# Layer 0 attention with the scores made twice: turned score products, maxima subtracted inside the product, sums from the value product

## The chip, the cores and the metric

The program runs on one core of a Trainium2 chip. Its time is the device time of one execution in microseconds (us). A core has TensorE (PE, whose weight loads are listed as PEld), VectorE (DVE), ScalarE (ACT), GpSimd (POOL) and SyncE (SP, which only starts transfers here). Each works through its own queue in order, and they meet at semaphores.

## What is computed

The reference is a stack of four layers, each `x + attention(norm(x)) + ffn(norm(x))`, on x of 4 batches of 256 rows of 512 values. Only layer 0's attention, and one small step of layer 1, are touched:

```python
q, k, v = (proj(wq), proj(wk), proj(wv))        # 32 heads of 16 values
q = _apply_rope(q, sin, cos)                    # x * cos + rot * sin
k = _apply_rope(k, sin, cos)
scores = jnp.einsum('bnth,bnsh->bnts', q, k) * (1.0 / math.sqrt(h))
scores = jnp.where(causal, scores, -jnp.inf)
attn = jax.nn.softmax(scores, axis=-1)
out = jnp.einsum('bnts,bnsh->bnth', attn, v)
out = out.transpose(0, 2, 1, 3).reshape(B, T, C)
return jnp.einsum('btc,dc->btd', out, wo)
```

Layer 1 needs for its "bind" vectors the mean magnitude of two small weight vectors per head (`alpha = mean(abs(w))`).

## The kernel before

Everything is in float32. A float32 product is two matrix instructions and two weight loads in the trace, so that a count of x8 there is four products.

**Blocks.** `layer0_attention` (L151) takes one batch of 256 rows after the other. In a batch, queries and keys stand as features on the partitions: four blocks of 128 features, that is 8 heads each, a pair of heads (e = 0 and 1) in each group of 32 partitions. There are 16 blocks. `kT` holds the keys twice, once with the features of the other head of each pair set to zero (`eo`, L286 and L287), so that one product with 32 contraction rows gives the scores of both heads of a pair; four such products, in the four row groups of the array, run together (L357). The causal mask makes three quarters of a square of scores: "part 1" is the lower 128 query rows against 256 keys, "part 0" the upper 128 against 128 keys.

**A head's path.** DVE adds the mask, negates and takes the minimum in one pass from PSUM to SBUF (`masked`, L379, which gives the negated maximum `nm`). ACT takes the exponential in place, with the sum of each row (L393). DVE inverts the sums (L404), POOL multiplies by them (L406), PE turns three 128x128 squares so that keys stand on the partitions (L417), DVE or ACT copies them out of PSUM (`keys`, L98 and L96), and PE multiplies by the values (L430), one group of 32 columns of the array for each pair, `v` having zeros in the columns of the other head. ACT copies the result of e = 0 to `oT` (L442) and DVE adds that of e = 1 (L444). Per block there are 8 such heads.

**Features.** For each block of queries and of keys: four products (L260), two multiplications with the rotary tables on DVE (L271), a product with a signed permutation `swap` that exchanges the two halves of a head (L275), an addition on DVE (L282), and for keys the two masked copies (ACT L286, DVE L287). Values are products L303, the output projection L327, the addition to x L337.

**Order.** The queues of PE, DVE, ACT and POOL are written by hand: a loop over slots h, 8 to a block, issues what is due, some of it through `at(h, ...)`. Features, values and the norm of the next batch (`turn`) are spread over the slots of the current one. `aside` holds 64 small pieces, one for each odd slot: the unpacking of the gate and up weights of layer 0's feed-forward part (L563 to L599, DVE, with transfers from SP). PSUM has 8 banks: 4 for scores (tag A), 2 for the turned squares (T), 2 for halves that everything else takes in turn (`hb`, L200).

**Layer 1's step.** At the end of layer 0's feed-forward part, `binding` (L811) fills a 128x128 square with ones on POOL (L815), takes magnitudes on ACT (L817) and adds them over the partitions with a product on PE (L819). On POOL's queue the fill stands behind two multiplications of the norm (L835).

Of the kernel before, what the change touches and what calls it, by code (L numbers as in the profile page):

```python
# [30 lines left out]
P = 128  # L31
# [24 lines left out]
def block_stack(ctx: ExitStack, tc: tile.TileContext, d: dict, out: bass.AP):  # L56
# [94 lines left out]
    def layer0_attention(hook, aside):  # L151
# [6 lines left out]

        with (
# [3 lines left out]
            psum_banks("ps_a0", A=4, T=2, H=2),  # L163
# [7 lines left out]
            swap = load(wp, "swap0", eng=nc.scalar)  # L171
# [9 lines left out]
            for i in range(2):  # L181
                v = wp.tile([P, 2, 2, L0_PAIRS, 32], F32, name=f"v0_{i}")
                nc.gpsimd.memset(v, 0.0)
                vbuf.append(v)
            hook()
# [8 lines left out]
            for t in range(2):  # L194
                turned(t, xns[t])
# [47 lines left out]
            class Batch:  # L243


                def __init__(self, b):
# [3 lines left out]
                    self.oT = ap.tile([P, NC, T], F32, tag="oT", name=f"oT_{b}")  # L250
                    self.v = vbuf[b % 2]

                def features(self, h, qk, blk):
# [18 lines left out]

                    def rotate():
                        had["rot"] = hb()
                        nc.tensor.matmul(had["rot"], lhsT=swap, rhs=had["qs"], start=True, stop=True)  # L275

                    def add():
                        if qk == 0:
                            dst = self.qT[:, blk, :]
                        else:  # L280
                            dst = had["kk"] = ap.tile([P, T], F32, tag="kk", name="kk" + name)
                        nc.vector.tensor_tensor(dst, had["rot"], had["qc"], ALU.add)  # L282

                    def split():
                        dst, kk = self.kT[:, blk], had["kk"]
                        nc.scalar.activation(dst[:, 0, :], kk, AF.Copy, scale=eo[:, 0:1])  # L286
                        nc.vector.tensor_scalar(dst[:, 1, :], kk, eo[:, 1:2], None, ALU.mult)  # L287
# [3 lines left out]
                    at(h + 3, rotate)  # L291
                    at(h + 4, add)
                    if qk:
                        at(h + 5, split)
# [49 lines left out]
            class Block:  # L344


                def __init__(self, u, blk):
                    self.u, self.blk = u, blk
                    self.p, self.keys = [], []

                def scores(self, part):
# [3 lines left out]
                    self.s = [ps("A", [P, 2, n], f"s{part}_{self.blk}_{i}") for i in range(4)]  # L355
                    for r, s in zip(rows, self.s):
# [8 lines left out]
                def masked(self, part, i):  # L365

                    if part:
                        self.p.append(
                            [
                                smp.tile([P, 2, T], F32, tag="p1", name="p1"),  # L370
                                smp.tile([P, 2, P], F32, tag="p0", name="p0", bufs=7),
                                smp.tile([P, 2, 2], F32, tag="nm", name="nm"),
                                smp.tile([P, 2, 2], F32, tag="sums", name="sums"),
                                smp.tile([P, 2, 2], F32, tag="rs", name="rs"),
                            ]
                        )
                    p1, p0, nm, _, _ = self.p[i]
                    for e in range(2):
                        nc.vector.tensor_tensor_reduce(  # L379
                            out=(p1 if part else p0)[:, e, :],  # L380
                            in0=self.s[i][:, e, :],
# [5 lines left out]
                            accum_out=nm[:, e, part : part + 1],  # L387
                        )

                def exponentials(self, e, i):  # L390
                    p1, p0, nm, sums, _ = self.p[i]
                    for part, p in ((1, p1), (0, p0)):
                        nc.scalar.activation(  # L393
                            p[:, e, :],
                            p[:, e, :],
                            AF.Exp,
                            bias=nm[:, e, part : part + 1],
                            scale=-1.0,
                            accum_out=sums[:, e, part : part + 1],
                        )  # L400

                def normalise(self, e, i):
                    p1, p0, _, sums, rs = self.p[i]
                    nc.vector.reciprocal(rs[:, e, :], sums[:, e, :])  # L404
                    for part, p in ((1, p1), (0, p0)):
                        nc.gpsimd.tensor_tensor(  # L406
                            p[:, e, :],
                            p[:, e, :],
                            rs[:, e, part : part + 1].to_broadcast([P, p.shape[2]]),
                            ALU.mult,  # L410
                        )

                def transpose(self, e, i):
                    p1, p0 = self.p[i][:2]
                    tp = ps("T", [P, 3, P], "pT")
                    for k, src in enumerate((p0[:, e, :], p1[:, e, 0:P], p1[:, e, P:T])):
                        nc.tensor.transpose(tp[:, k, :], src, ident)  # L417
                    self.turned = tp

                def copied(self, e, i):  # L420
                    self.keys.append(smp.tile([P, 3, P], F32, tag="keys", name="keys"))
                    evac(i, self.keys[-1], self.turned)

                def values(self, e):

                    v = self.u.v
                    av = hb()
                    for k, cols, of in ((0, slice(0, T), slice(0, 2)), (1, slice(P, T), slice(2, 3))):
                        for i, r in enumerate(rows):
                            nc.tensor.matmul(  # L430
                                av[r, cols],
# [1762 lines left out]
```

## Time and profile before

| | |
|---|---|
| Median of 3 runs | 1456.17 us (1454.14 to 1458.66) |
| The profiled execution | 1458.98 us, span of its instructions 1457.1 us, mean granted TensorE clock 0.983 |
| Layer 0 attention | from the start to 301.0 us, where the first instruction of the feed-forward part (ACT L685) starts |
| Busy in the first 300 us | PE 262.2, DVE 209.8, ACT 164.2, POOL 133.9 us |
| Busy in the whole span | PE 1381.7, DVE 910.3, ACT 571.1, POOL 737.1 us |
| Layer 1's step | PE waits 3.97 us before L819, at 455.94 us |

A row of a group of instructions has the line, the engine, the operation, output and inputs by the program's names with their shapes, the count, busy time and mean duration of one, and the idle time of the engine just before them with what ended it. Neighbouring instructions of an engine overlap at their ends: in a dense stretch the distance from start to start is less than the mean duration, and the timeline shows it. A row of the timeline has start, duration, engine, line, operation, shapes and a count of merged instructions; a bracket gives the wait before it.

### The profile page before, as it was taken

What the parts mean: (1) busy time and instruction counts of PE and PEld (TensorE: products, weight loads), DVE (VectorE), ACT (ScalarE), POOL (GpSimd) and SP (SyncE); (2) the same over time, 40 slices, a digit from 0 to 9 for tenths busy, and PEclk for the clock granted to TensorE, in tenths of its full rate; (3) what the DMA queues carried; (4) which work ended last, traced back from release to release, by engine and by line L of the source; (5) the groups of instructions that cost most, each with busy time, mean ns of one, the idle gap of its engine ahead of it and who ended that gap; (6) DMA issues with size and microseconds to landing.
All of it is one profiled execution on the core that took longest, in us unless ns stands there. A gap on an engine that the chain in (4) does not pass through costs nothing.

```text
span 1457.1 us, 21158 instructions
## 1 busy us (share of the span) xinstructions
PE 1381.7 (95%) x7204; PEld 1085.1 (74%) x7204; DVE 910.3 (62%) x2482; ACT 571.1 (39%) x1717; POOL 737.1 (51%) x790
## 2 busy tenths in 40 slices
PE   7988989899998999999999999999999999989998
PEld 4656656578644657887887888888888788777887
DVE  5687777768844437745556765566565555857654
ACT  2565656768401222312332333323333233445430
POOL 1354535657751204755575776857757666310200
PEclk9999999999999999999999999999999999999999
DMA  5021112220250002210121202211022010302001
GB/s 191 1 57 34 42 30 42 59 75 1 69 144 0 15 0 89 64 45 24 61 88 42 75 26 65 89 48 62 23 87 87 29 30 0 131 1 109 1 1 58
DMA packets 50958, 76.23 MB, mean 52 GB/s; under 512 B 16491, under 2 KB 23942, under 8 KB 50466
## 3 DMA queue, kind: packets, MB, share of 16 engines
q1 hardware_dynamic: 49778, 73.77, 16.8%
q8 instruction: 57, 0.93, 0.3%
q10 hardware_dynamic: 960, 0.85, 0.2%
q0 software_dynamic: 112, 0.26, 0.1%
q14 instruction: 51, 0.42, 0.1%
HBM read 66.96 MB, written 7.91 MB: 51 GB/s over the span
## 4 chain that ended last, share of the span: by engine, by line
PE 79%; DVE 13%; ACT 3%; issue 2%; POOL 1%; DMA 1%; SPq 0%; ACTq 0%; DVEq 0%; POOLq 0%
PE m L1301 15%; PE m L1265 14%; PE dn L665 5%; PE gu L699 4%; PE half L260 4%; PE s L1645 4%; PE av L1718 4%; PE m L1287 3%; PE m L1277 3%; PE s L357 2%; PE pT L417 2%; PE s L1649 2%; PE l1o L948 2%; PE av L1719 2%; PE half L327 2%
## 5 line engine op out<-in xcount | busy, mean ns | idle before, releaser
L1693 POOL TENSOR_TENSOR p<-p,rs 128x512 f32<-128x512 f32 (+1 forms) x128 | 107.5, 860 | 242.8 <-DVE rs L1690 242.8
L406 POOL TENSOR_TENSOR p<-p,rs 128x256 f32<-128x256 f32 (+1 forms) x256 | 129.2, 529 | 156.6 <-DVE rs L404 131.3
L1711 ACT COPY q<-pT 128x512 f32<-128x512 f32 x64 | 37.5, 585 | 280.5 <-PE pT L1702 280.5
L1679 ACT ACTIVATE p<-p,nm 128x256 f32<-128x256 f32 (+1 forms) x256 | 113.3, 451 | 54.4 <-DVE nm L1663 54.4
L1690 DVE RECIPROCAL rs<-sums 128x4 f32<-128x4 f32 x64 | 11.4, 178 | 178.2 <-ACT p L1679 177.9
L393 ACT ACTIVATE p<-p,nm 128x256 f32<-128x256 f32 (+1 forms) x256 | 113.6, 449 | 0.9 <-DVE nm L379 0.9
L1265 PE MATMUL m<-xT,wq_b 128*128 128x256 f32 x448 | 103.9, 380 | 4.4 <-DVE x_sb L1515 3.0
L379 DVE CUSTOM_DVE_ANT_0 p<-s,cmask 128x256 f32<-128x256 f32 (+1 forms) x256 | 79.0, 347 | 38.2 <-PE s L357 33.8
L1265 PEld LDWEIGHTS m<-xT,wq_b 128*128 128x128 f32 x448 | 82.1, 190 | 14.8 <-DVE x_sb L1515 3.4
L1248 POOL TENSOR_TENSOR c<-c,z 128x512 f32<-128x512 f32 x28 | 36.4, 1298 | 111.0 <-DVE c L1247 41.7
L1301 PE MATMUL m<-wo_b,o 128*128 128x256 f32 x384 | 90.2, 381 | 0.0
L1317 POOL TENSOR_TENSOR q<-q,t 128x512 f32<-128x512 f32 x64 | 85.2, 1333 | 6.1 <-DVE t L1316 6.1
L1316 DVE TENSOR_TENSOR t<-m,rope_sb 64x512 f32<-64x512 f32 (+1 forms) x144 | 86.3, 600 | 1.9
L1350 DVE TENSOR_TENSOR x_sb<-x_sb,m 128x512 f32<-128x512 f32 x82 | 54.5, 680 | 50.8 <-PE m L1301 40.7
L665 PE MATMUL dn<-wd,hT 128*128 128x512 f32 x176 | 80.6, 619 | 2.3 <-DVE sb L714 2.3
L1663 DVE CUSTOM_DVE_ANT_0 p<-s,cmask 128x256 f32<-128x256 f32 (+1 forms) x256 | 76.1, 353 | 10.6 <-PE s L1645 8.3
L1265 PE MATMUL m<-x_s,wq_t 128*128 128x256 f32 x320 | 78.4, 391 | 3.3 <-DVE x_sb L1350 2.2
L417 PE MATMUL pT<-ident,p 128*128 128x128 f32 x384 | 66.0, 288 | 15.6 <-ACT keys L96 6.6
L1301 PEld LDWEIGHTS m<-wo_b,o 128*128 128x128 f32 x384 | 70.8, 190 | 10.8 <-DVE t L1316 2.3
L1727 ACT COPY o<-av 128x512 f32<-128x512 f32 x64 | 37.6, 588 | 90.9 <-PE av L1719 90.7
L417 PEld LDWEIGHTS pT<-ident,p 128*128 128x128 f32 x384 | 44.9, 145 | 36.8 <-POOL p L406 21.1
L1265 PEld LDWEIGHTS m<-x_s,wq_t 128*128 128x128 f32 x320 | 61.7, 196 | 13.4 <-DVE x_sb L1350 2.6
(322 smaller groups left out, 3557.9 us busy)
## 6 DMA issues: line engine op xcount, KB each, us to landing
wq_b<-in_wq SPq DMA_DIRECT2D x38, 256.0 KB
wo_b<-in_wo SPq DMA_DIRECT2D x32, 256.0 KB
raw<-in_wo SPq DMA_DIRECT2D x16, 512.0 KB
wkv_b<-in_wkv SPq DMA_DIRECT2D x16, 256.0 KB
wos_d<-wos_row SPq DMA_DIRECT2D x28, 128.0 KB
gate_q<-in_gate_q SPq DMA_DIRECT2D x11, 256.0 KB
up_q<-in_up_q SPq DMA_DIRECT2D x11, 256.0 KB
wq3s_b<-in_wq SPq DMA_DIRECT2D x8, 256.0 KB
```

The costliest lines, as they stand in the source:

```text
L379: nc.vector.tensor_tensor_reduce(out=(p1 if part else p0)[:, e, :], in0=self.s[i][:, e, :], in1=cmask if part else cmask[:, P : 2 * P], sc ...
L393: nc.scalar.activation(p[:, e, :], p[:, e, :], AF.Exp, bias=nm[:, e, part : part + 1], scale=-1.0, accum_out=sums[:, e, part : part + 1],)
L406: nc.gpsimd.tensor_tensor(p[:, e, :], p[:, e, :], rs[:, e, part : part + 1].to_broadcast([P, p.shape[2]]), ALU.mult,)
L417: nc.tensor.transpose(tp[:, k, :], src, ident)
L665: nc.tensor.matmul(po, lhsT=hT[:, k, t * P : (t + 1) * P], rhs=wd[:, k, :], start=k == 0, stop=k == NBLK - 1,)
L1265: nc.tensor.matmul(out[:, i, :], lhsT=b[:, c, i * P : (i + 1) * P], rhs=a[:, c, :], start=start and i == 0 and c == 0, stop=i == 1 and c == 1,
L1301: nc.tensor.matmul(out[:, t, :], lhsT=a[:, c, t * P : (t + 1) * P], rhs=b[:, c, :], start=start and t == 0 and c == 0, stop=t == 1 and c = ...
L1316: nc.vector.tensor_tensor(t2[at], src[of], sin[of], ALU.mult)
L1317: after(1, lambda: nc.gpsimd.tensor_tensor(dst, dst, t2, ALU.add))
L1663: nc.vector.tensor_tensor_reduce(out=x[f"p{part}"][:, e, :], in0=x[f"s{part}"][:, e, :], in1=cmask if part else cmask[:, P : 2 * P], scale ...
L1679: nc.scalar.activation(p, p, AF.Exp, bias=x["nm"][:, part, e : e + 1], scale=-1.0, accum_out=x["sums"][:, part, e : e + 1],)
L1693: nc.gpsimd.tensor_tensor(p, p, bc(x["rs"][:, part, :], 2, n), ALU.mult)
```

## The change

The exponentials are no longer taken in the layout in which the maxima are found. Scores are still made as before, but only for their maxima; then they are made a second time with keys on the partitions, less the maxima, and the exponential of that is what the value product takes.

- The two `masked` passes (DVE) remain, but their output is thrown away (tile `masked`); the negated maximum goes to a column of one of three 128x256 tiles `maxima`, at row 16 of a pair's 32 for head 0 and at row 0 for head 1.
- `widened`: ACT makes `q_e`, the block's queries twice, each with the other head's features set to zero (2 x 128x256); POOL makes `k_e`, the keys `kT` with a one added in row 16 (head 0) or row 0 (head 1) of each 32 (128x512).
- `turn_maxima`: PE turns the two 128x128 squares of maxima into one half; `lowered`: DVE puts them, by a mask, into the free row of `q_e` (2 x 128x256). The product of `k_e` and `q_e` then is score less maximum.
- `turned`: for each e four products of 256 columns and four of 128 in the four row groups, into four PSUM tiles of 128x384. `exponentials`: one ACT pass 128x384 from PSUM for each head, straight into `keys`. `selected`: POOL sets the entries above the diagonal to zero (two 128x128 squares in one instruction per head).
- The value buffers are filled with ones instead of zeros, so the value product gives the row sums in the columns of the other head. `gathered` takes by a mask the outputs (`o_e`) and the sums, on ACT for e = 0 (2 x 128x256) and on DVE for e = 1 (2 x 128x256). `inverted`: DVE inverts 128x256 sums and exchanges the 16s of each 32 with a stream shuffle; `normalised`: POOL multiplies (128x256). The per-head reciprocal, multiplication, three squares and copy are gone.
- The rotary exchange is a stream shuffle on DVE (128x256) instead of the product with `swap`, whose load is gone; the signs move to the table; the addition moves from DVE to POOL; the second masked copy of keys moves from DVE to ACT.
- PSUM: six banks for scores of both kinds (A=6), none for squares. Each block takes 16 banks from A instead of 8.
- The loop is written anew: offsets of a block's steps from its slot 8n are in two tables, features of the next batch keep their slots, three of batch 0's features and its values move a few slots, and the outputs of batches 1 and 2 are put together after slot 106 (of 134), those of batch 3 at the end. The 64 pieces of `aside` still go to the odd slots from 1.
- In layer 1 the fill with ones and the magnitudes move from `binding` to `values_binding`, where they are issued earlier on POOL and ACT.

```diff
-            psum_banks("ps_a0", A=4, T=2, H=2),
+            psum_banks("ps_a0", A=6, H=2),
...
-                nc.gpsimd.memset(v, 0.0)
+                nc.gpsimd.memset(v, 1.0)
...
+                        nc.vector.stream_shuffle(had["rot"], had["qs"], [i ^ 8 for i in range(32)])
...
-                        nc.vector.tensor_tensor(dst, had["rot"], had["qc"], ALU.add)
+                        nc.gpsimd.tensor_tensor(dst, had["rot"], had["qc"], ALU.add)
...
+                        for e in range(2):
+                            nc.scalar.activation(dst[:, e, :], kk, AF.Copy, scale=eo[:, e : e + 1])
...
+                def widened(self):
+                    for e in range(2):
                         nc.scalar.activation(
+                            self.q[:, e, :], self.u.qT[:, self.blk, :], AF.Copy, scale=eo[:, e : e + 1]
                         )
+                    nc.gpsimd.tensor_tensor(
+                        self.k, self.u.kT[:, self.blk], bc(eo[:, 2:4], 2, T), ALU.add
+                    )
...
+                def lowered(self):
+                    for e in range(2):
+                        q = self.q[:, e, :]
+                        nc.vector.scalar_tensor_tensor(
+                            q, self.maxT, eo[:, 2 + e : 3 + e], q, ALU.mult, ALU.add
+                        )
...
+                def turned(self, e):
+                    self.st = [ps("A", [P, 3, P], f"st_{self.blk}_{i}") for i in range(4)]
+                    for k, of in ((0, slice(0, 2)), (1, slice(2, 3))):
+                        for r, s in zip(rows, self.st):
+                            nc.tensor.matmul(
+                                s[:, of, :],
+                                lhsT=self.k[r, e, k * P : k * P + P],
+                                rhs=self.q[r, e, k * P : T],
+                                start=True,
+                                stop=True,
+                            )
+                def exponentials(self, i):
+                    self.keys.append(smp.tile([P, 3, P], F32, tag="keys", name="keys", bufs=9))
+                    nc.scalar.activation(self.keys[-1], self.st[i], AF.Exp)
+                def selected(self, e, i):
+                    k = self.keys[4 * e + i][:, 0:3:2, :]
+                    nc.gpsimd.affine_select(
...
+                def inverted(self):
+                    nc.vector.reciprocal(self.sums, self.sums)
+                    nc.vector.stream_shuffle(self.sums, self.sums, [i ^ 16 for i in range(32)])
...
+            first = {
+                -10: lambda x: x.scores(1),
+                -6: lambda x: x.scores(0),
+                -3: lambda x: x.turn_maxima(),
+                -2: lambda x: x.lowered(),
+                0: lambda x: x.turned(0),
+                4: lambda x: x.turned(1),
+                6: lambda x: x.values(0),
+                7: lambda x: x.gathered(0),
+                10: lambda x: x.values(1),
+                11: lambda x: x.gathered(1),
+                13: lambda x: (x.inverted(), x.normalised()),
+            }
+            then = {
+                -9: lambda x: (x.masked(1, 0), x.masked(1, 1)),
+                -8: lambda x: x.masked(1, 2),
+                -7: lambda x: (x.masked(1, 3), x.widened()),
+                -5: lambda x: (x.masked(0, 0), x.masked(0, 1)),
+                -4: lambda x: (x.masked(0, 2), x.masked(0, 3)),
+            }
...
+            self.full = lp.tile([P, P], F32, name="full")
+            nc.gpsimd.memset(self.full, 1.0)
+            self.mag = lp.tile([P, 2, H], F32, name="mag")
+            nc.scalar.activation(self.mag, w["bqk"], AF.Abs)
             self.vbind = signs(lp, w["bv"], alpha, [P, H, P], "v").rearrange("p h d -> p (h d)")
...
-            full = lp.tile([P, P], F32, name="full")
-            nc.gpsimd.memset(full, 1.0)
-            mag = lp.tile([P, 2, H], F32, name="mag")
-            nc.scalar.activation(mag, w["bqk"], AF.Abs)
```

## The prediction, as put on record before the changed kernel ran

> **What bounds the kernel now.** I read the page first (PE 95% busy), then busy times by stretches of 20 us, then the groups by shape, the waits and the timeline. Layer 0 attention ends at 301.0 us, where ACT L685 starts. Its stretches, with columns start:end, length, busy PE, PEld, DVE, ACT, POOL, granted clock, DMA share, GB/s:
>
> ```profile
> 140.00:160.00 20.00, 18.70 (x137) 13.42 (x130) 16.25 (x77) 13.02 (x51) 10.27 (x20) 1.00 0.19 42
> 160.00:180.00 20.00, 18.53 (x145) 12.91 (x145) 15.49 (x75) 12.09 (x51) 10.31 (x21) 1.00 0.18 38
> 180.00:200.00 20.00, 17.09 (x115) 12.20 (x114) 12.13 (x56) 10.39 (x40) 7.66 (x16) 0.91 0.17 40
> ```
>
> PE leads, DVE follows at three quarters, DMA is idle. What PE does is in the groups of the first 460 us:
>
> ```profile
> L406 POOL TENSOR_TENSOR p<-p,rs 128x256 f32<-128x256 f32 x128 | 79.2, 619 | 156.6 <-DVE rs L404 131.3 <-PE pT L417 15.4 <-ACT v L314 4.7
> ...
> L417 PE MATMUL pT<-ident,p 128*128 128x128 f32 x384 | 66.0, 288 | 15.6 <-ACT keys L96 6.6 <-DVE keys L98 6.4 <-DVE rs L404 0.8
> ...
> L404 DVE RECIPROCAL rs<-sums 128x2 f32<-128x2 f32 x128 | 19.8, 154 | 2.3 <-ACT p L393 2.1
> ...
> L275 PE MATMUL half<-qs,swap_sb 128*128 128x256 f32 x64 | 19.6, 388 | 1.4 <-DVE qT L282 0.9 <-DVE qc L271 0.4
> ```
>
> PE spends 66 us on squares and waits for their POOL, DVE and ACT neighbours; POOL waited 157 us. Because instructions overlap, I cost them from start to start, from PE's timeline:
>
> ```profile
> 153.97 1.14 PE L357 MATMUL s<-kT,qT 32*128 32x512 f32 x8
> 155.05 0.86 PE L430 MATMUL half<-keys,v 128*32 128x256 f32 x16
> 155.84 1.21 PE L417 MATMUL pT<-ident,p 128*128 128x128 f32 x6
> 156.88 1.89 PE L260 MATMUL half<-xT,wq_sb 128*128 128x256 f32 x8
> 158.61 0.49 PE L417 MATMUL pT<-ident,p 128*128 128x128 f32 x3
> ```
>
> So: scores of part 1 take 1.07 (155.05 less 153.97), of part 0 (the row at 161.63, next at 162.27) 0.64, a value product 0.79, a square 0.165 to 0.173 (six in 1.04), a full product of four 1.73. In the same way DVE: a masked pass 0.345 (256) or 0.21 (128), an operation 128x256 with a PSUM input 0.33, a keys copy 0.47, a small reciprocal 0.08. POOL: 0.97 for L406's two; ACT: 0.38 for a copy of 384 from PSUM, 0.40 to 0.42 for a pass over 256.
>
> **PE per block.** Removed: 24 squares 3.96 and two swap products 0.87. Added: the second scores. Their 256-column groups are part 0's, 0.64. Four of 128 columns are not in the trace; 1.07 less 0.64 is 0.43 per 256 columns, so 0.64 less 0.21 gives 0.43 (ends 0.35, half of a value product's rest, and 0.64). Twice 1.07 makes 2.14, two squares of maxima 0.33. Net -2.4, from 15.3 to 13.0 on average.
>
> **DVE per block.** Removed: 8 reciprocals 0.64, 4 copies 1.88, 2 rotary additions 0.66, one masked key copy 0.27, oT 0.33: 3.8. Added: `lowered` 0.66, `gathered` 0.66, three shuffles, one reciprocal over 256. A shuffle is not in the trace; the nearest row, L287 with SBUF on both sides, has 0.27: I take 0.30 (ends 0.27 and 0.47, a copy of 384). The reciprocal is the large unknown. At the low end it is like any pass over 256, 0.33. But its own rows grow: 128x2 154, 128x4 178, 128x8 203 ns, that is 6 to 8 ns an element where a tensor operation from 128x4 (153) to 128x8 (167) has about 3. Over 256 that makes 1.6 to 2.2; I take 1.9. Added 4.1, net +0.3, from 12.1 to 12.4. DVE comes level with PE.
>
> **ACT and POOL.** ACT loses 8 x 0.88 and 4 x 0.38 and the oT copy, and gains 8 exponentials from PSUM at about 0.43, q_e 0.84, a key copy 0.42, gathered 0.74: from some 10 to 7. POOL loses 8 x 0.97 and gains 8 selections, the nearest row being
>
> ```profile
> L931 POOL TENSOR_SCALAR_AFFINE_SELECT a<-a 128x256 f32<-128x256 f32 x16 | 6.9, 453 | 31.9 <-ACT a L930 31.9
> ```
>
> so 3.6, k_e 1.3 (L1033, 128x512) and three operations of 0.6: 6.7. Here a rule of the Trainium skill speaks against the change: "GPSIMD Engine Reference", section "4.1 Engine selection", wants elementwise work on VectorE and not on GpSimd, which is slower for two inputs. The rows agree on the price (619 against 416 ns of L282). By the rule the three operations would stay on DVE, 1.0 more in each of 16 blocks; by the rows POOL has half its time free, and a feature is wanted two slots later or more. I go with the rows: cost nothing. Were POOL late, `split` would wait on ACT, with exponentials queued behind it and PE's next scores waiting for their bank.
>
> **The sum by intervals.** Work is uneven: features and values (1.73 on PE; 0.96 or 0.2 on DVE) fall on odd slots of some blocks, on top of 5.8 on PE and 8.0 plus 2.1 of weight pieces on DVE for each. I cut both queues of the changed program where a block's first part-1 scores stand, for intervals 1 to 14 (PE/DVE): 10.8/9.7, 11.6/12.0, 7.5/10.0, 10.9/11.8, 13.3/13.4, 13.3/13.2, 12.7/11.6, 12.7/11.9, 13.3/13.0, 13.3/13.9, 7.5/10.4, 10.9/11.8, 12.7/11.0, 9.2/11.3. The larger sum to 170. The same method on the kernel before gives 209, while the trace has 237 (about 28.5 to 266.0): 28 more, of which some 12 is clock (the share not granted, times length, over the stage) and 16 is handing over, 1.2 an interval.
>
> Handing over after: walking one feature block by hand, in order, PE first waits 0.9 for the masked passes before the squares of maxima, but DVE then sets the pace: 14.0 against 13.9. A block with one product takes about 11 against 10.1, as exponentials on ACT and bank releases bind. There are fewer hops than before but two equal queues; I take 1.0, 14 in all.
>
> Clock: here the Trainium skill and the trace part. Rows (as above):
>
> ```profile
> 114.00:116.00 2.00, 0.40 (x2) 0.15 (x2) 2.00 (x9) 0.01 (x1) 0.97 (x2) 1.00 0.04 8
> 116.00:118.00 2.00, 1.83 (x9) 1.55 (x10) 0.70 (x6) 1.35 (x6) 0.97 (x2) 0.71 0.45 137
> 118.00:120.00 2.00, 2.00 (x6) 1.32 (x4) 0.00 (x0) 0.77 (x4) 0.00 (x0) 0.50 0.37 60
> ```
>
> PE was thin, not idle, and the clock fell to half. "TensorE: Matmul & The Clock Gate", "Part 1: The HAM clock gate", has it fall after an idle window of some 3.4 us. By that rule the new stage, whose waits are near 1 us, loses nothing; by the rows each thin stretch costs about 2.5. Thin are intervals 3, 11 and 14: 7.5.
>
> Start: without swap products in between, the four first features end near 19.5; keys are ready by 19.6 (end of the second feature 16.1, rotary 1.0, a norm statistic 0.7, POOL 0.6, two ACT copies 0.8, handovers 0.4), so first scores at 20.3 for 23.2, interval 0 takes 10.7: 31. Tail from the last block's scores: before 35 us for 29.7 of PE work. After 29.3, but the end is a chain: last values, gathered 0.7, reciprocal and shuffle 2.2, POOL 0.6, then output products 6.9 and addition: 35 again. The weight pieces keep their slots, and their transfers with them; DVE waited 0.8 for the first (`gate_q`, started at 77.3, taken at 82.7), and with slots a fifth shorter may wait 1 to 2 there, which PE's slack in interval 3 mostly covers. Stage end: 31 + 170 + 14 + 7.5 + 35 = 257.5, a gain of 43.5.
>
> **Layer 1's fill.**
>
> ```profile
> 435.50 16.47 PE L665 MATMUL dn<-wd,hT 128*128 128x512 f32 x38
> 455.94 0.59 PE L819 MATMUL alpha<-mag,full 128*128 128x8 f32 x2 [3.97 <-POOL full L815]
> 456.39 7.97 PE L665 MATMUL dn<-wd,hT 128*128 128x512 f32 x12
> ...
> 465.07 5.32 PE L665 MATMUL dn<-wd,hT 128*128 128x512 f32 x12
> ```
>
> The fill stood behind two POOL multiplications; issued earlier it lies among the weight additions before 421 us, and ACT is idle for 52 us before 444. PE saves 3.97, and the next twelve run in 5.32 for 7.97: 6.6. Late next would be the squares of the normed rows, ready at 453.0, wanted at 457.5: nothing. Low end 4.0. After layer 0 all orders else are the same and PE is the bound, so gains pass on.
>
> Profiled execution: 1458.98 less 50.1 is 1408.9. It lies 2.8 above the median; so 1406.
>
> **Rivals.** (a) The reciprocal costs 0.33: PE alone binds, intervals sum to 162, the tail loses 1.6, together 9 less: 1397. For it: no row above 8 elements; against it: the slope. (b) Handing over costs twice as much, 2.2 an interval and 4 in the tail: the ring of six banks makes each group of four scores wait for two banks that DVE frees and two that ACT frees, four times a block, and PE and DVE have no slack for each other. 21 more: 1427. For it: before, PE with slack on DVE lost 1.2; against it: the walk. (c) Slower: half-filled, row-tiled scores now make up more of PE's work, and the clock stays low. To lose, the stage must end past 307.6, so intervals average 17.2 for 13.7. With 11.4 of PE work and 1 of handing over each, PE would be at half clock 60% of the time, as against 8% now. At 65% it gives 1466. Against it: at 54 to 56 us PE did nothing but such products at clock 1.00. (d) PE and DVE alternate, the stage gains nothing and the fill its low end 4.0: 1452.
>
> **Chances.** Main case 0.60, its own range 1396 to 1417; (a) 0.13; (b) 0.20; (d) 0.03; (c) 0.04. Faster by over 0.3% (about 4.4 us, what a measurement tells from no change) 0.93, same 0.03, slower 0.04. The range 1388 to 1432 takes in (a), (b) and the fill's low end.
>
> **What would show it.** First scores near 20, stage end near 257; second scores of 1.07 a group in place of L417's squares; DVE busy near 90% in 40 to 220; a reciprocal 128x256 of 1.6 to 2.2; no wait before alpha. The forecast is wrong if granted clock falls in the stage, if PE's waits for DVE and ACT exceed 30 us, or if a shuffle or selection takes over 1 us.

## The result and the profile after

The changed kernel takes 1438.16 us (median of 4 runs, 1435.28 to 1438.68) against 1456.9 for the kernel before beside it: a ratio of 0.9869, 95% interval 0.9848 to 0.9890. It is faster, by 1.3% and not by the 3.4% of the forecast, and lies 6 us above the top of its range. The profiled execution took 1438.15 with a span of 1436.4 (before: 1458.98 and 1457.1).

Layer 0's attention ended at 301.0 us and now ends at 287.2, where ACT L732 starts. That is a gain of 13.8 for a forecast of 43.5. What follows went from 1156.1 to 1149.2: 6.9 for a forecast of 6.6. The whole miss lies in the attention. Its stretches after, with the columns of those shown before:

```profile
140.00:160.00 20.00, 17.33 (x149) 11.39 (x149) 16.74 (x66) 7.08 (x18) 8.58 (x15) 1.00 0.16 41
160.00:180.00 20.00, 18.27 (x145) 12.43 (x144) 16.38 (x63) 7.12 (x19) 7.68 (x13) 1.00 0.20 41
180.00:200.00 20.00, 16.62 (x150) 11.10 (x150) 19.05 (x83) 9.17 (x23) 11.59 (x20) 0.97 0.17 41
```

PE is less busy than before and DVE busier, and neither is full. The new groups in the first 300 us:

```profile
L433 POOL TENSOR_SCALAR_AFFINE_SELECT keys<-keys 128x256 f32<-128x256 f32 x128 | 56.8, 456 | 108.5 <-ACT keys L429 102.4 <-POOL keys L433 2.8 <-issue 1.4
...
L419 PE MATMUL st<-q_e,k_e 32*128 32x256 f32 x256 | 40.1, 439 | 9.0 <-DVE maxima L376 6.6 <-ACT keys L429 2.2
...
L473 DVE RECIPROCAL sums<-sums 128x256 f32<-128x256 f32 x16 | 28.0, 1748 | 0.0
...
L281 DVE STREAM_SHUFFLE rot<-qs 128x256 f32<-128x256 f32 x32 | 14.0, 438 | 0.0
```

The reciprocal takes 1.75 us (forecast 1.6 to 2.2), a selection 0.46. POOL's additions and products, 0.73 to 0.83 for 0.6, are furthest from their price. What stands between them is in the list of PE's waits from 19 to 290 us (us in total, times, longest):

```profile
PE half L404 <- DVE maxima L376: 10.3, 10, 1.6
PE st L419 <- DVE maxima L376: 6.6, 9, 1.2
PE half L308 <- DVE v L320: 3.6, 3, 1.4
PE half L268 <- DVE qc L279: 3.0, 5, 0.7
```

PE stands before the squares of maxima (L404) and before second scores (L419), each time for DVE's passes over scores. The waits in the stage that DVE and ACT ended, these and smaller ones, sum to about 31 us (26.5 before), past the 30 that the forecast had named as a sign of being wrong. One such place, from the changed kernel's timeline (start, length; in brackets the idle time before and what ended it):

```profile
148.97 0.71 PE L363 MATMUL s<-kT,qT 32*128 32x256 f32 x8
...
149.61 1.99 PE L268 MATMUL half<-xT,wk_sb 128*128 128x256 f32 x8
...
150.80 0.28 DVE L376 CUSTOM_DVE_ANT_0 masked<-s,cmask 128x128 f32<-128x128 f32 x1
151.53 0.94 PE L419 MATMUL st<-q_e,k_e 32*128 32x256 f32 x16
151.64 0.42 DVE L279 TENSOR_TENSOR qs<-half,rope_sb 128x256 f32<-128x256 f32 x1 [0.55 <-PE half L268]
...
152.65 0.28 DVE L376 CUSTOM_DVE_ANT_0 masked<-s,cmask 128x128 f32<-128x128 f32 x1
...
153.28 0.29 DVE L376 CUSTOM_DVE_ANT_0 masked<-s,cmask 128x128 f32<-128x128 f32 x1
...
153.63 0.44 PE L404 MATMUL half<-ident,maxima 128*128 128x128 f32 x2 [1.16 <-DVE maxima L376]
```

At about 151.0 DVE is through with half of its part-0 passes. The scores for the other half (148.97) have been there since 149.7, but the rotary of L279 comes first in DVE's order, and its product (149.61) ends only at 151.6. DVE idles 0.55, turns for 1.0, makes the four passes, and PE, which needs the last of them, idles 1.16. DVE waits for PE and then PE for DVE, in one slot.

**PE's own work and the rest.** To see the sum, I priced every group on PE by its start-to-start time where nothing waits (product 1.725, second scores 0.86, part-1 scores 1.00, part-0 scores 0.645, value product 0.785, square 0.165, swap product 0.43, squares of maxima 0.275, square of a normed row 0.13), took off the clock that was not granted (its share times length), and called what is left the excess: waits, changes of tile shape, slow starts. From the first scores to the start of the last batch's output products:

| kernel | length | priced work | clock | excess |
|---|---|---|---|---|
| before | 270.4 | 226.6 | 11.9 | 31.9 |
| changed | 255.8 | 183.1 | 11.9 | 60.8 |

The work left PE as it should, 43.5. The excess took back 28.9. Half of the new excess, 30.6, lies at the second scores: from the start of a group to whatever PE does next, less 0.86 and the clock.

### The profile page after: what moved, and what is told of

It is laid out like the page before. It is cut to its first block, busy times and chain, and to the rows that moved or that the text cites. A ratio compares the mean times of both kernels' runs of the same rounds, so it can differ in the third digit from the quotient of the medians.

```text
span 1436.4 us, 20830 instructions
## 1 busy us (share of the span) xinstructions
PE 1360.0 (95%) x7300; PEld 1065.0 (74%) x7300; DVE 923.1 (64%) x2402; ACT 509.3 (35%) x1333; POOL 718.5 (50%) x729
## 4 chain that ended last, share of the span: by engine, by line
PE 69%; DVE 10%; ACT 2%; issue 1%; POOL 1%; DMA 0%; SPq 0%; ACTq 0%; DVEq 0%; POOLq 0%
PE m L1348 16%; PE m L1312 14%; PE dn L712 5%; PE gu L746 4%; PE s L1692 4%; PE av L1765 4%; PE m L1334 3%; PE m L1324 3%; PE s L1696 2%; PE l1o L995 2%; PE av L1766 2%; DVE t L1363 2%; PE half L332 1%; PE pT L1749 1%; PE pT L1748 1%
## 5 line engine op out<-in xcount | busy, mean ns | idle before, releaser
L1758 ACT COPY q<-pT 128x512 f32<-128x512 f32 x64 | 37.5, 586 | 280.4 <-PE pT L1749 280.4
L1726 ACT ACTIVATE p<-p,nm 128x256 f32<-128x256 f32 (+1 forms) x256 | 113.4, 451 | 54.3 <-DVE nm L1710 54.3
L433 POOL TENSOR_SCALAR_AFFINE_SELECT keys<-keys 128x256 f32<-128x256 f32 x128 | 56.8, 456 | 108.5 <-ACT keys L429 102.4
L429 ACT ACTIVATE keys<-st 128x384 f32<-128x384 f32 x128 | 57.5, 488 | 78.0 <-PE st L419 78.0
L1710 DVE CUSTOM_DVE_ANT_0 p<-s,cmask 128x256 f32<-128x256 f32 (+1 forms) x256 | 76.1, 354 | 10.8 <-PE s L1692 8.4
L376 DVE CUSTOM_DVE_ANT_0 masked<-s,cmask 128x256 f32<-128x256 f32 (+1 forms) x256 | 76.2, 351 | 1.5 <-PE s L363 1.3
L766 POOL TENSOR_TENSOR sa<-sa,sb 128x1024 f32<-128x1024 f32 x22 | 62.1, 2826 | 18.4 <-DVE sb L761 18.4
L1765 PE MATMUL av<-q,kv 128*128 128x512 f32 x128 | 66.5, 602 | 0.0
```

The lines of the kernel that those rows point to most:

```text
L376: nc.vector.tensor_tensor_reduce(out=ap.tile([P, T], F32, tag="masked", name="masked")[:, 0:n], in0=self.s[part][i][:, e, :], in1=cmask if ...
L429: nc.scalar.activation(self.keys[-1], self.st[i], AF.Exp)
L766: nc.gpsimd.tensor_tensor(self.a, self.a, self.b, ALU.add)
L1710: nc.vector.tensor_tensor_reduce(out=x[f"p{part}"][:, e, :], in0=x[f"s{part}"][:, e, :], in1=cmask if part else cmask[:, P : 2 * P], scale ...
L1726: nc.scalar.activation(p, p, AF.Exp, bias=x["nm"][:, part, e : e + 1], scale=-1.0, accum_out=x["sums"][:, part, e : e + 1],)
L1765: nc.tensor.matmul(av, lhsT=v[:, 0:P], rhs=x["q0"], start=True, stop=False)
```

## The experiments

Each kernel was timed in 4 runs with a profile, the ring of five in 12. The granted clock moves a run by up to 20 us, so two more numbers are given for each: the time not granted (span times 1 less the mean granted clock) and the full-clock span (span times clock), both medians over the runs. The ratio is to the kernel before on the same chip, with its interval.

| kernel | us | ratio | not granted | full-clock span |
|---|---|---|---|---|
| before (in each set) | 1455.9 to 1458.3 | 1 | 20.3 to 23.3 | 1432.9 to 1433.9 |
| changed | 1438.2 | 0.9869 (0.9848 to 0.9890) | 23.0 | 1413.5 |
| 1 rotary turn alone | 1436.3 | 0.9866 (0.9847 to 0.9886) | 22.9 | 1410.8 |
| 2 all but the turn | 1446.7 | 0.9942 (0.9920 to 0.9965) | 19.5 | 1426.8 |
| 3 no reciprocal | 1437.4 | 0.9868 (0.9825 to 0.9911) | 31.6 | 1404.1 |
| 4 maxima later | 1441.3 | 0.9906 (0.9887 to 0.9925) | 22.3 | 1417.3 |
| 5 part-0 passes first | 1436.4 | 0.9870 (0.9846 to 0.9894) | 25.1 | 1408.9 |
| 6 ... and values in two tiles | 1437.7 | 0.9866 (0.9833 to 0.9899) | 29.4 | 1405.5 |
| 7 ... and logarithm on ACT | 1471.3 | 1.0108 (1.0081 to 1.0135) | 37.5 | 1432.1 |
| 8 turn and fill | 1429.0 | 0.9814 (0.9791 to 0.9837) | 20.0 | 1407.8 |
| 9 all passes first | 1429.9 | 0.9808 (0.9778 to 0.9839) | 25.7 | 1402.3 |
| 10 ... and value copies on ACT | 1429.9 | 0.9809 (0.9764 to 0.9853) | 28.6 | 1401.0 |
| 11 ... and no reciprocal | 1417.2 | 0.9718 (0.9680 to 0.9755) | 22.7 | 1393.1 |
| 12 as 10, power on POOL | 2043.1 | 1.4014 (1.3978 to 1.4050) | | |
| 13 as 9, ring of five | 1455.7 | 1.0000 (0.9982 to 1.0018) | 32.0 | 1422.2 |
| 14 as 9, products in pairs | 1482.9 | 1.0172 (1.0150 to 1.0194) | 56.3 | 1424.9 |
| 15 as 14, fewer pairs | 1471.2 | 1.0095 (1.0072 to 1.0117) | 49.2 | 1419.5 |

**1, 2 and 8: which part pays.**

```diff
# 1, in the kernel before (2 is the reverse edit in the changed kernel, rotate at h + 2)
-   had["rot"] = hb()
-   nc.tensor.matmul(had["rot"], lhsT=swap, rhs=had["qs"], start=True, stop=True)
+   nc.vector.stream_shuffle(had["rot"], had["qs"], [i ^ 8 for i in range(32)])
-   nc.vector.tensor_tensor(dst, had["rot"], had["qc"], ALU.add)
+   nc.gpsimd.tensor_tensor(dst, had["rot"], had["qc"], ALU.add)
# 8 is 1 with full and mag made in values_binding
```

> The kernel before, with the rotary turn alone changed: half turn by shuffle, addition on POOL, both key copies on ACT (no second scores, no sums from value products, layer 1's fill where it was). Theory 1 (PE bounds the attention before, so what leaves PE is gained): 0.87 us of swap products leave PE in each of 16 blocks, 14 us, and the early start of the first scores comes with it; 1443 to 1446. Theory 2 (the scores part is what shortens the changed kernel and the turn only shifts work): within 3 us of the kernel before, 1454 to 1457.

> The changed kernel with the old rotary turn (swap product on PE, addition on DVE, one key copy on DVE): second scores, sums from value products and layer 1's fill stay. Theory 1 (after the change PE and DVE are both nearly full and wait for each other, so that the score part gives back on DVE and in tile changes what it takes from PE): the score part alone is worth little; with the fill's 6.6 the time is 1446 to 1454. Theory 2 (the score part carries the gain): 1438 to 1442, as the changed kernel.

> The kernel before with the rotary turn by shuffle and layer 1's fill moved, without the score part. If the parts add, the turn's 20 us and the fill's 6.6: 1429 to 1431, and so the score part costs some 8 us where it stands. If the fill is worth nothing there: 1436.

The turn alone is worth 19.6 us, more than the 14 of theory 1 and as much as the whole change. In its profile PE has 12.1 less priced work than before (28 swap products) and 4.4 less excess; the first scores come 3.4 earlier, and the clock happened to take 3.4 less. The fill adds its 7.3 (1436.3 to 1429.0). So the score part, which was to bring most, costs 8 to 9 us where it stands (1429.0 to 1438.2; 8.0 by the ratios), 5.7 of it at full clock. With PE's groups priced as above, from run 8 to the changed kernel, priced work goes from 214.5 to 183.1 and the excess from 26.1 to 60.8. The score part takes 31 from PE and gives back 35.

With the old turn (run 2, as theory 1 had it) the score part and the fill gain 9.2, so the score part alone about 2. The parts do not add: 19.6 and 9.2 would make 28.8, and together they bring 18.7.

**3 and 4: DVE's amount, or PE's wait.**

```diff
# 3: the normalisation is left out
-   nc.vector.reciprocal(self.sums, self.sums)
# 4: out of first, behind the slot's products and rotary
    then = { ...
+       -3: lambda x: x.turn_maxima(),
+       -2: lambda x: x.lowered(),
```

> The changed kernel without its reciprocal of the sums (128x256, 1.75 us on DVE in each block); values are multiplied by the turned sums, so the normalisation is left out. Theory 1 (DVE is nearly full and PE waits for its passes over the scores): most of 16 x 1.75 = 28 us leaves DVE, of which PE, near 13 us a block with its tile changes, lets about half show: 1420 to 1428. Theory 2 (PE sets the pace by tile changes, clock and the wait for the maxima, DVE has room): under 4 us, 1434 to 1438.

> The changed kernel with the squares of maxima issued behind the projection product of the same slot and the addition of the maxima to the queries behind that slot's other work, so that PE does not stand at the squares for DVE's last passes (1.2 us in most blocks). Theory 1 (DVE sets the pace with PE): PE's waits at the squares vanish but turn up at the next thing DVE owes; gain 0 to 6, 1432 to 1438. Theory 2 (PE's own waits set the pace): 9 waits of 1.2 and those like them, 11 to 18 us: 1420 to 1427.

Run 3 took nothing off the time. It lies in the range of theory 2, but only through the clock: at full clock it saves 9.4, and the clock takes 8.6 more. Its PE waits for the maxima just as long, with 28 us less on DVE:

```profile
PE half L404 <- DVE maxima L376: 10.2, 10, 1.5
PE st L419 <- DVE maxima L376: 6.5, 9, 1.2
```

So those waits do not come from the amount on DVE, though the amount costs something elsewhere. Run 4 is slower than both figures: it moved the wait and did not end it. The squares wait little (1.2 in all), but what stands behind them waits for the addition of the maxima:

```profile
PE half L308 <- DVE q_e L409: 9.5, 3, 3.3
PE half L268 <- DVE q_e L409: 7.1, 6, 1.8
```

What is left is the order on DVE, as the place at 151 us shows.

**5 and 9: the passes ahead.** Only the order on DVE changes, part 0 in run 5, both parts in run 9:

```diff
    first = { ...
+       -9: lambda x: (x.masked(1, 0), x.masked(1, 1)),
+       -8: lambda x: x.masked(1, 2),
+       -7: lambda x: x.masked(1, 3),
+       -5: lambda x: (x.masked(0, 0), x.masked(0, 1)),
+       -4: lambda x: (x.masked(0, 2), x.masked(0, 3)),
```

> The changed kernel with one thing moved: DVE's passes over the part-0 scores are issued ahead of the rotary and copies of their slot, not behind them; PE's order is the same instruction for instruction. Theory 1 (the loss is order: DVE stands at a rotary whose product PE has not finished while the passes that PE will wait for lie behind it): most of the 17.9 us that PE waits for the maxima goes, 8 to 16 us at an equal clock: 1422 to 1430. Theory 2 (DVE's load: whatever comes first, the next thing that DVE owes is late, as when the squares were put later): within 4 us, 1434 to 1440.

> The changed kernel with all of DVE's passes over scores, of both parts, ahead of the rotary and copies of their slot. In the run with the part-0 passes first, the wait for the maxima had gone, but a second-score group and what follows it still took 24 us over 32 x 0.86, of which 8 stood inside the groups behind DVE's part-1 passes, which free the banks. Theory 1 (order and the ring of six banks): these 8 go too; at an equal clock 4 to 8 us less than with part 0 alone, full-clock span 1400 to 1404, time 1426 to 1434 according to the clock. Theory 2 (a fixed cost of the groups, not order): no change from 1436, full-clock span 1408.

Run 5's list of PE's waits:

```profile
PE st L419 <- DVE maxima L376: 6.3, 8, 1.2
...
PE half L404 <- DVE maxima L376: 2.2, 5, 0.8
```

The wait at the squares falls from 10.3 to 2.2, and the full-clock span by 4.6, between the two figures; most of that is hidden in the time by the clock. With part 1 ahead too (run 9, as theory 1 had it), the time falls to 1429.9 and the full-clock span by 11.2 in all. The excess at second scores goes from 30.6 to 23.2 and 17.0. Order is the largest single term that a run took away. How the second step works is not fully shown: PE's named waits at second scores only fall from 6.3 to 5.4 in it, and passes made earlier also free their banks earlier, so order and ring are not told apart there.

**6, 7, 10, 11, 12: taking work off DVE.**

```diff
# 6: v as two tiles, one for each e      # 10: the odd copy
-   nc.vector.tensor_copy(self.v[:, 1, ...], pv[:, :, 1, :])
+   nc.scalar.copy(self.v[:, 1, ...], pv[:, :, 1, :])
# 7 (with 5 and 6)
-   nc.vector.reciprocal(self.sums, self.sums)
+   nc.scalar.activation(self.sums, self.sums, AF.Ln)
+   nc.scalar.activation(self.sums, self.sums, AF.Exp, scale=-1.0)
# 11 (with 10): no reciprocal, normalisation left out    # 12: after the shuffle
+   nc.gpsimd.tensor_tensor(self.sums, self.sums, minus.to_broadcast([P, T]), ALU.pow)
```

> As the run with the passes first, and the values kept in two tiles, one for each half of the heads, so that DVE's copy of the odd heads no longer waits for ACT's copy of the even ones (9.7 us of DVE's idle time, 3.6 of PE's, in intervals 1 to 14 of the changed kernel). Theory 1 (waits by order and by shared tiles make the loss): 3 to 7 us less than with the passes first alone. Theory 2 (DVE's load or PE's own work): no more than 2 us less.

> As the run with all passes first, and both value copies on ACT. Keeping the values in two tiles did not take away DVE's wait for ACT's copy (12.1 us)[...]. Theory 1 (DVE's idle time there is passed on to PE): DVE loses 16 x 0.2 of work and most of the 12 us of waiting: 4 to 8 us less than the run before at an equal clock. Theory 2 (DVE has room): within 2 us.

> As the run before, with the reciprocal of 128x256 (1.75 us on DVE a block) replaced by a logarithm and an exponential of its negative on ACT, which is idle more than half of the time. Theory 1 (once order is mended DVE's amount, 12 us of some 14 a block, is next): 4 to 10 us less than the run before. Theory 2 (PE's work with tile changes and the clock sets the pace): within 3 us of it. If ACT loads a table for each block, 2.6 us in each, exponentials come late and it is slower.

> As the run before without the reciprocal (the normalisation is left out), as a floor for what DVE's load still costs once order is mended. Theory 1 (after mending, DVE's 12 us of some 14 a block bind): 6 to 10 us less at an equal clock. Theory 2 (PE, tile changes and banks bind): within 3 us at an equal clock. Either way the granted clock is watched: without the reciprocal alone the time not granted was 17 to 37 us for 20 to 23; if a thin PE lowers it, it is above 23 here too.

> As the run with all passes first and both value copies on ACT, with the reciprocal taken from DVE and made on POOL as the power -1 of the turned sums (a two-operand operation over 128x256, then the product as before). Without any reciprocal that kernel took 1417. Theory 1 (DVE's load costs 8 to 13 us once order is mended, POOL has half its time free): if the power takes no more than some 3 us on POOL, 1417 to 1423. Theory 2 (the normalised values come later by POOL's longer turn and the last block's outputs wait for it): the reciprocal's latency moves, 1426 to 1432; if the power takes over 6 us, POOL's selections come late and it is slower than 1432.

Two tiles took nothing from DVE's wait for ACT's value copy (12.1 us with and without), so sharing the tile was not its cause. One engine for both copies ends it, but gains only 1.3 at full clock; what made DVE wait there is not shown. The reciprocal, once order is mended, costs 12.7 (7.9 at full clock) of its 28. That is no more than at the old order, where run 3 saved 9.4 at full clock. The two ways tried to make it elsewhere are worse. The Trainium skill ("ScalarE: Activation LUTs", "Table sets: the hidden batching unit") lists a set that holds both functions, which would need no load between them. In run 7 ACT loads a table before each of the two in every block (14 blocks lie in the stretch of these rows), and DVE waits 48.1 us in all for the sums:

```profile
L473 ACT ACT_TABLE_LOAD x14 | 18.0, 1283 | 0.2
L474 ACT ACT_TABLE_LOAD x14 | 18.0, 1283 | 0.2
```

And a power on POOL takes 41 us for one tile:

```profile
L478 POOL TENSOR_TENSOR sums<-sums,minus 128x256 f32<-128x256 f32 x16 | 658.6, 41165 | 3.6 <-DVE sums L475 3.6
```

**13, 14 and 15: the ring of banks, and products in pairs.**

```diff
# 13
-   psum_banks("ps_a0", A=6, H=2)
+   psum_banks("ps_a0", A=5, H=2)
# 14: two products in one slot, likewise for values and the other features
-   u.features(h0 + 2 * i, i % 2, i // 2)
+   u.features(h0 + 4 * (i // 2), i % 2, i // 2)
# 15: the last two features of a batch again one to a slot
-   u.features(h0 + 28, i, 3)
+   u.features(h0 + 28 + 2 * i, i, 3)
```

> The run with all passes first, with a ring of five banks for scores instead of six. There, 20 us over 32 x 0.86 still stand at the second-score groups, with visible waits for DVE's passes and ACT's exponentials. Theory 1 (the ring is what ties PE to DVE and ACT: each group of four needs banks that the group before it has just filled): with five, three of the four come from the group just before; 10 us or more slower at an equal clock, full-clock span over 1412. Theory 2 (six are enough, the rest is tile changes and order): within 4 us, full-clock span 1400 to 1406.

> The run with all passes first, with projection products of batches 1 to 3 issued two to a slot instead of one to every second slot, so that 8 products of each of three batches have a product of the same tile shape beside them (at most 12 pairs of each 2 x 8 tiles, 24 changes of 0.095 us less, 2.3 us). Theory 1 (a tile change costs what PE's pitches say, and products need not be spread): 2 to 4 us less at an equal clock, full-clock span 1398 to 1401. Theory 2 (spread products are what PE does while DVE and ACT work; two together leave it with nothing in the next slot): 3 us or more slower, full-clock span over 1405, and a lower granted clock.

> As the run with products in pairs, but the last two feature products of each batch stay one to every second slot: in that run they took product halves that still held transposed rows not yet copied, so part of the rows of batches 2 and 3 was overwritten, and its time may hold waits of that. 9 pairs are left instead of 12. Theory 1 (a tile change costs 0.095 and products need not be spread): 1 to 3 us less than the run with all passes first at an equal clock, full-clock span 1399 to 1401. Theory 2 (spread products are the work that PE does while DVE and ACT catch up, pairs leave its next slot bare): 8 to 22 us more, full-clock span 1410 to 1425, with more time not granted than 26 us.

A bank less costs 19.9 at full clock and 25.8 in time. PE's waits in run 13:

```profile
PE s L363 <- ACT keys L429: 12.4, 9, 2.0
PE st L419 <- DVE maxima L376: 11.4, 17, 2.3
```

Both are waits of a score group for a bank. So PE is tied to DVE and ACT through the ring. What six banks cost against more is not shown: all eight are in use.

Pairs are much slower, with rows overwritten (14) or not (15): 17.2 at full clock and 23.5 more not granted in run 15. Both runs came out as theory 2: the products are what PE does while DVE and ACT catch up. Without one in the slot, PE stands:

```profile
92.61 0.71 PE L363 MATMUL s<-kT,qT 32*128 32x256 f32 x8
93.15 0.60 PE L419 MATMUL st<-q_e,k_e 32*128 32x256 f32 x4
96.25 2.06 PE L419 MATMUL st<-q_e,k_e 32*128 32x256 f32 x12 [2.50 <-DVE maxima L376]
98.24 0.69 PE L404 MATMUL half<-ident,maxima 128*128 128x128 f32 x2
98.72 5.79 PE L308 MATMUL half<-wv_sb,xT 128*128 128x256 f32 x16
```

After the wait of 2.50, the pair of products takes 5.7 where two take 3.5 at full clock. The cost of a change of tile shape can't be read from these runs. It rests on the trace alone.

## Why the prediction was wrong

The step that failed is "Handing over after: ... I take 1.0, 14 in all". It was 31.4. Of the 17.4 that were missed there, the order in which DVE works off a slot made 8.6; the rest is explained only in part. Against the sum, in us:

| term | predicted | measured |
|---|---|---|
| up to scores of the second block | 31 | 32.3 |
| intervals 1 to 14, larger of PE and DVE | 170 | (170) |
| handing over in them | 14 | 31.4 |
| clock in them | 7.5 | 11.9 |
| from the last block's scores to the end | 35 | 41.6 |
| end of the attention | 257.5 | 287.2 |
| layer 1's fill | 6.6 | 6.9 |

(Intervals 1 to 14 took 213.3; 213.3 less 170 less 11.9 is 31.4.)

**Handing over** was 2.2 an interval, the price of rival (b), which got a chance of 0.20. Its mechanism, the ring, ties the engines (run 13), but that its size of six is the first cause is not shown. The largest part that a run took away is the order in which DVE makes its passes: 11.2 of full-clock span (run 9). I had walked one feature block "in order", found 0.9 before the squares of maxima and let it go because "DVE then sets the pace". But DVE itself stood idle in that slot, for the product that PE had been given late. A wait on each side cannot be covered by the other side's load. The kernel before issues the passes ahead of a slot's rotary and copies, the changed one behind them. The two loops show that, and the forecast did not cost it.

Order is not all of it. With the clock taken off, from one trace each (good to about 2 us):

| kernel | intervals 1 to 14 | from there to the end |
|---|---|---|
| forecast | 184 | 35 |
| changed | 201.4 | 39.9 |
| 3 no reciprocal | 196.0 | 35.4 |
| 9 all passes first | 192.8 | 37.2 |
| 10 ... and value copies on ACT | 188.8 | 37.5 |
| 11 ... and no reciprocal | 185.2 | 33.7 |

Of the 17.4 us missed in the intervals, order gave back 8.6. Run 11 comes near the 184, but its own floor is lower: by the sum of rival (a), without the reciprocal's weight on DVE, it is 162, so handing over is still about 23 there. What makes that rest stays open.

**DVE as an equal queue** was half right. Its work was as forecast: shuffle 0.33 from start to start (0.30), reciprocal 1.75 (1.9), the addition of maxima 0.40 (0.33), busy 176.9 of 213.3 us or 83% (near 90%). Run 3 shows that this did not make the waits for maxima. Runs 3 and 11 show that the reciprocal costs 8 to 9 at full clock in either order, and by the table above about half of that lies in the tail.

**PE per block** had two errors of opposite sign. Second scores take 0.86, not 1.07: part-1 scores were the wrong model for the 256-column group with four of 128. And projection products, which I left at 1.73, take 1.92:

```profile
145.39 0.94 PE L419 MATMUL st<-q_e,k_e 32*128 32x256 f32 x16
146.25 1.99 PE L268 MATMUL half<-xT,wq_sb 128*128 128x256 f32 x8
148.18 0.86 PE L449 MATMUL half<-keys,v 128*32 128x256 f32 x16
148.97 0.71 PE L363 MATMUL s<-kT,qT 32*128 32x256 f32 x8
```

146.25 to 148.18 is 1.93. Before, a product lay between squares of the same tile shape, 128*128, at 1.73; with one neighbour of another shape 1.82, here with two 1.92. Each change beside a product costs 0.095 (the Trainium skill, "TensorEngine Tiling (Array Packing)", "Key Properties", has TensorE drain at a change of tiling, without a price). From the first scores to the last outputs there are 91 such changes in place of 27: 6 us lost, beside 32 x 0.2 gained at second scores. That the two nearly cancel is luck. The squares that were removed had made products cheap.

**Clock.** 11.9 against 7.5. In the intervals the changed kernel's trace has the clock at half in four stretches: from 45.07 (6.83 us long), 55.31 (3.41), 75.79 (6.83) and 198.67 (6.83). Half of these 23.9 us is the 11.9. Of the thin intervals that I named, 3 and 11 came, at 3.4 each and not 2.5, and 14 did not; the other 5.1 fell in intervals 1 and 2. The 3.41 us before each of the four (columns as above):

```profile
41.66:45.07 3.41, 2.08 (x14) 1.24 (x15) 3.41 (x21) 1.28 (x3) 2.71 (x3) 1.00 0.00 0
51.90:55.31 3.41, 3.07 (x21) 2.02 (x20) 3.41 (x20) 2.28 (x6) 0.63 (x2) 1.00 0.02 5
72.38:75.79 3.41, 1.98 (x10) 0.88 (x10) 3.41 (x10) 2.20 (x6) 3.04 (x5) 1.00 0.07 14
195.26:198.67 3.41, 2.42 (x28) 1.40 (x18) 3.30 (x18) 3.09 (x8) 3.02 (x6) 1.00 0.00 0
```

PE was busy for most of them, but work on the whole array (128*128) made up 0.9 us of the second and nothing of the others; the rest was scores and value products, each on a part of the array. In all kept traces but run 12's, 12 to 320 us, half clock followed 119 of 1239 such stretches at full clock. All 28 with under 1.5 us of busy PE are among the 119, but so are 91 others. Columns of products, weighted by the share of the array that they use, tell them apart better: under 1472, the bound that parts them best (full products without a pause make about 4050) lie 98 of the 119 and 14 of the 1120 others. No run varied this alone, so it is a correlation and not a cause shown.

So what rival (c) feared is there, but small: the share not granted from the first scores to the last outputs is 4.7% (11.9 of 255.8) for 4.4% before. (The stretch that I held against it, 54 to 56 us, ends in squares from 55.73 on.) Most of the kernels with less on DVE or a mended order lose no less (23 to 32 us over a whole run in runs 3, 5, 6, 9, 10 and 11). In run 10 (columns as above, 1.7 us each):

```profile
39.70:41.40 1.70, 1.33 (x12) 0.68 (x10) 1.31 (x7) 0.41 (x2) 1.44 (x4) 1.00 0.00 0
41.40:43.10 1.70, 0.00 (x0) 0.00 (x0) 1.70 (x3) 0.47 (x2) 1.70 (x2) 0.95 0.00 0
43.10:44.80 1.70, 1.16 (x9) 1.20 (x12) 1.70 (x17) 0.81 (x3) 0.67 (x2) 0.50 0.00 0
```

PE waited 2.60 us for DVE's passes here, and the clock fell to half. That is less than the idle window of some 3.4 us of the Trainium skill ("TensorE: Matmul & The Clock Gate", "Part 1: The HAM clock gate"), so the rows, not the rule, were the ones to go by. Run 15's place, 2.50 us of waiting and then slow products, is of the same kind. What exactly makes it fall stays open: the kernel without the reciprocal lost 17 us in one run and 37 in another.

**Tail.** 41.6 for 35. The chain was as described, and PE stood 2.65 for it:

```profile
279.50 7.57 PE L332 MATMUL half<-wo_sb,oT 128*128 128x256 f32 x26 [2.65 <-POOL oT L477]
```

Of the 6.6 too many, 1.7 is clock. The rest is waits for maxima and for the addition to the queries between the last blocks, as in the intervals. With all passes first the tail was 37.2.

**POOL.** That additions on GpSimd cost nothing is not contradicted: in run 1, where they stand on POOL, the turn gains more than the swap products' time. They were not tried alone.

**Fill.** Right in size and place. Layer 1's row product (L866) waits for nothing and the next twelve products run at full clock:

```profile
438.08 0.28 PE L866 MATMUL alpha<-mag,full 128*128 128x8 f32 x2
438.22 5.40 PE L712 MATMUL dn<-wd,hT 128*128 128x512 f32 x12
```

**The turn** (run 1) was undersized: it was counted as 0.87 of PE work a block, and PE's waits for DVE around the swap products were not. Before, they came to 5.0 us (3.7 ahead of the next product, 1.3 ahead of the swap product), and in run 1 they are gone.

In the end two ways beat the changed kernel: the turn and the fill without the score part (run 8, 1429.0), and the score part with its passes first (run 9, 1429.9; run 10 the same). They can't be told apart in time; at full clock the second is 5.5 ahead, which its clock takes back.

## What to carry to other kernels

When two engines come level, the sum of the larger queue is a floor, and the order inside a slot is one of the things that decide how far above it the time lands: put what another engine waits for ahead of what itself waits for that engine. Look for a slot in which A waits for B and then B for A; taking 28 us of work off one of them left the wait as it was here, and moving a few lines ended most of it. Price an operation with its neighbours (a product between other tile shapes is dearer by a tenth), and compare variants at equal clock before reading small differences.

## What the runs showed of the hardware

A power on GpSimd over 128x256 takes 41.2 us, 161 ns for each element of a row; the product of the same size beside it takes 0.72. A logarithm and an exponential in turn loaded a table each time, 1.28 us (run 7). A reciprocal on VectorE over 128x256 takes 1.75 us, four times a tensor operation of 0.42. Products of 32 rows start four at a time (145.39 to 145.41, then 145.71 to 145.73), a group of sixteen instructions in 0.86 us. A change of tile shape on TensorE costs 0.095 us beside a full product. In the changed kernel's attention the half clock lasts 3.41 or 6.83 us at a time.
